# Two expert layers: the overflow branch ahead of the tiles, the last tile mixed in by a product with a matrix of weights, the first tile's rows of the first layer by one-hot products

## The chip, the cores and the metric

The kernel runs on one core of a Trainium2 chip. The metric is the device time of one execution in microseconds (us). The engines are PE (matrix products; PEld is its loading of the stationary operand), DVE (vector operations), ACT (activations and copies, and a queue for transfers), POOL (here mostly gathers of rows) and SP (issues loads of weights). Each runs its own instructions in order and waits on the others through semaphores. 16 DMA engines move the data.

## The reference

The program is a residual stack on x (256 tokens by 768): four pairs of a graph layer and a feed-forward layer, each as x = x + layer(layernorm(x)). Only two feed-forward layers are touched. Both are mixtures of eight experts of which each token uses two:

```python
# L1_ffn, "first expert layer"
topk_vals, topk_idx = jax.lax.top_k(xf @ Wr.T, 2)
routing_weights = jax.nn.softmax(topk_vals, axis=-1)
h = jnp.einsum('th,efh->etf', xf, Wi) + bi[:, None, :]        # 768 -> 384
expert_out = jnp.einsum('etf,ehf->eth', gelu(h), Wo) + bo[:, None, :]
out = sum of routing_weights * expert_out over the token's two experts

# L2_ffn, "second expert layer"
w, idx = gate(xt, gate_w, gate_b)                              # two of eight, in groups
g = swiglu((x @ W1 + B1) * (x @ W3 + B3))                      # 768 -> 768 -> 384
out = sum of w * (g @ W2 + B2) over the token's two experts + shared_ffn(xt)
```

`shared_ffn` has the form of one more expert that every token uses.

## The kernel before

256 tokens with two experts each are 512 rows. Each expert computes only its own rows. How many an expert gets is known only at run time, so the experts are ranked by load (`ranked`, line 992) and put into a fixed set of tiles of 128 rows: `TILES1` (line 1189) has seven, `TILES2` (line 1190) six. Each entry is (rank, first row, rows): the most loaded expert has 192 rows, some tiles are shared by two experts of 64 rows. `plan` (line 966) gives for each rank where its rows begin (base), how many fit (room) and where they go if they don't (jump). Rows that don't fit go to further tiles, "more", which are computed only when some expert has more rows than room: the overflow branch, a `tc.If` on a number read from memory. With the given inputs it isn't taken.

`dispatch` (line 1024) works out on DVE the row number of each of a token's two experts (`places`), the matrix `is_e` of which expert has which rank, and hands back a function `rest` (line 1052) for what can wait: row numbers as integers, the two weights, the overflow flag. `find` (line 1076) turns this round: a one-hot matrix `hot` compares the row numbers with a count (four DVE operations), and PE products with the tokens' numbers give for each row of a tile its token (`slots`). `take` gathers the rows of a tile from a copy of the normalized x in DRAM (indirect DMA on POOL, `take_rows`, line 1101), and `tile_t` (line 1104) transposes them on PE.

The tiles then run in a loop (lines 1397 to 1414 for the first layer, 1623 to 1640 for the second). In one turn: the up products of tile u, the transposes of the activations of tile u-1 (`turned`), the transposes of tile u+1's rows, the down products of tile u-1 (`finish`, line 1162), whose result y goes to DRAM (`ys`) by ACT's queue (line 1165). All expert products are recorded at line 1117, in `by_parts`. Weights come in pieces of 1152 KB into a ring of eight buffers: `stream` (line 1170) with `pump` and `done` issues on SP (line 87) as many loads as there are free buffers. The expert's number is read from memory by SP (`nth`, line 1167). The second layer's W2 has a ring of three buffers of its own ("down").

After the loop: the last tile's `finish`; the expert's bias products (line 1419 in the first layer, `down_t`, lines 1095 and 1097, for the shared expert and the biases in the second) with `add_acc` (line 1324) into x; the overflow branch (lines 1423 and 1650); and `add_rows` (line 1127): four gathers from `ys` (two experts, two halves of the tokens), each multiplied by its weight and added to x (line 1134), and the layer norm of the next layer (lines 150 to 160). Then the next graph layer starts with transposes (line 171). After the second expert layer this graph layer also loads a small matrix `bd` by ACT's queue (line 1673), multiplies it on DVE (lines 1682, 1684) and uses it in `ps_a` (line 1692).

In the second layer the shared expert's up products (`up_shared(0)`, `(1)`, `(2)`; lines 102 and 1504 to 1513) stand ahead of the loop, between the steps of routing.

The order on each engine follows from the program by a scheduler that goes by priorities and ready times; products marked by `pin` keep the program's order among themselves. Across a `tc.If` nothing is moved: all that stands before it in the program is issued before it, all that stands behind it after it.

## Time and profile before

| | us |
|---|---|
| median of 4 runs (lowest, highest) | 1452.5 (1447.61, 1455.6) |
| the profiled execution: time | 1452.53 |
| its span in the profile | 1450.7 |
| PE busy in the span | 1246.9 |
| DVE, ACT, POOL busy | 665.2, 474.3, 357.2 |
| first expert layer: from its first tile's products to the next layer's first transpose | 861.69 to 948.54 |
| second expert layer: the same | 1095.36 to 1258.63 |

A line of the timeline gives the start in the span and the duration of an instruction or of a run of like ones (x is their number), the engine, the line of the kernel, the operation, the tile written, the tiles read, and their shape; in brackets how long the engine was idle before it and what ended that. A q behind the engine's name is its sequencer, which issues transfers and branches. An f32 product is recorded as two instructions. The table by stretches gives the granted clock of PE as a share of full speed and the mean share of the 16 DMA engines that was busy.

### The profile page before, as it was taken

How to read it: one execution, taken by the hardware profiler on the slowest of the kernel's cores; microseconds unless marked ns; L12 is line 12 of the kernel's file. 1: busy time of each engine (PE TensorE's matmuls, PEld its weight loads, DVE VectorE, ACT ScalarE, POOL GpSimd, SP SyncE). 2: the span in 40 equal slices, each digit the busy share in tenths (PEclk: the TensorE clock that was granted, in tenths of full speed). 3: DMA queues.
4: the chain of work that ended last, by engine and by line, in shares of the span. 5: the costliest groups of instructions: out<-in, count | busy, mean ns of one | idle time of the engine just before them, and what ended most of it. 6: DMA issues, size and time to landing. Idle time of an engine off the chain costs nothing. (4 is left out here: it accounts for less than half of the span.)

```text
span 1450.7 us, 13873 instructions
## 1 busy us (share of the span) xinstructions
PE 1246.9 (86%) x5047; PEld 768.8 (53%) x5068; DVE 665.2 (46%) x1251; ACT 474.3 (33%) x822; POOL 357.2 (25%) x195
## 2 busy tenths in 40 slices
PE   7999999789997884998989859676899999377998
PEld 4576444347643432855555445345486554166964
DVE  4321999930099996164352530166341101346023
ACT  1013877611287662241231112124111111153113
POOL 1001999900099991000203010111001000100000
PEclk9999999989999995999999969887989999665899
DMA  9323250205230023233632169461039995700000
GB/s 333 131 94 102 61 159 6 98 33 196 98 99 0 1 98 116 85 115 138 247 113 76 66 231 391 185 242 33 23 130 354 380 403 213 290 7 34 33 0 22
DMA packets 77930, 197.15 MB, mean 136 GB/s; under 512 B 9084, under 2 KB 24000, under 8 KB 77728
## 3 DMA queue, kind: packets, MB, share of 16 engines
q1 hardware_dynamic: 69088, 162.28, 31.1%
q0 software_dynamic: 6304, 27.94, 5.5%
q10 hardware_dynamic: 2464, 5.96, 1.1%
q8 instruction: 44, 0.72, 0.2%
q14 instruction: 30, 0.25, 0.1%
HBM read 177.84 MB, written 14.87 MB: 133 GB/s over the span
## 5 line engine op out<-in xcount | busy, mean ns | idle before, releaser
L784 POOL TENSOR_TENSOR gate<-gate,qT 128x2048 f32<-128x2048 f32 x64 | 287.7, 4531 | 241.7 <-ACT gate L764 241.3
L769 DVE TENSOR_REDUCE qiT<-gate 128x32 f32<-128x2048 f32 x96 | 215.0, 2279 | 16.2 <-POOL gate L784 15.1
L764 ACT ACTIVATE gate<-gate_acc,bg 128x1024 f32<-128x1024 f32 x192 | 209.6, 1113 | 38.2 <-PE gate_acc L760 35.5
L759 PE MATMUL gate_acc<-sela,ga 128*128 128x512 bf16 x363 | 139.3, 384 | 25.2 <-ACT gate L764 24.5
L760 PE MATMUL gate_acc<-selb,gb 112*128 112x512 bf16 x384 | 147.8, 385 | 1.2
L1117 PE MATMUL up_acc<-w_e,xgT 128*64 128x384 f32 (+1 forms) x432 | 96.5, 489 | 0.0
L760 PEld LDWEIGHTS <-gb 112*128 112x128 bf16 x384 | 37.6, 98 | 96.2 <-issue 71.3
L791 DVE TENSOR_TENSOR gate<-gate,ps_qy 128x2048 f32<-128x2048 f32 x32 | 72.9, 2278 | 0.2 <-ACT gate L764 0.2
L1117 PEld LDWEIGHTS up_acc<-w_e,xgT 128*64 128x64 f32 (+1 forms) x432 | 46.8, 154 | 44.9 <-issue 27.3
L171 PE MATMUL ps_tr<-ident,xn 128*128 128x128 f32 x84 | 18.0, 381 | 53.6 <-DVE ln_rs L158 27.0
L759 PEld LDWEIGHTS <-ga 128*128 128x128 bf16 x384 | 37.8, 98 | 47.8 <-issue 2.2
L642 PE MATMUL ps_alpha<-w_qb,qiT 128*128 128x384 f32 x96 | 44.1, 553 | 19.8 <-DVE qiT L769 19.8
L1101 POOL DMA_INDIRECT yg<-ys,rows x8 | 7.6, 953 | 196.6 <-PEq L1650 137.2
L566 DVE TENSOR_TENSOR ps_hg<-ps_hg,hg 128x384 f32<-128x384 f32 x8 | 4.5, 562 | 107.9 <-ACT hg L565 107.9
L326 PE MATMUL ps_pt<-ident,gat_z 128*128 128x128 f32 x104 | 24.2, 370 | 30.4 <-DVE gat_s L318 30.4
L457 PE MATMUL ps_z<-w_rel,xT 128*128 128x384 f32 x144 | 47.9, 486 | 0.0
L457 PE MATMUL ps_z<-w_rel,nT 128*128 128x384 f32 x144 | 47.5, 489 | 0.0
L461 ACT COPY z<-ps_z 128x384 f32<-128x384 f32 x24 | 11.5, 478 | 104.4 <-PE ps_z L457 104.4
L171 PEld LDWEIGHTS ps_tr<-ident,xn 128*128 128x128 f32 x84 | 14.5, 198 | 58.4 <-issue 33.5
L267 DVE CUSTOM_DVE_ANT_0 gat_dot<-xl,row 128x128 f32<-128x128 f32 (+2 forms) x56 | 23.8, 424 | 46.6 <-ACT xl L1471 18.9
L152 ACT ACTIVATE ln_rs<-ln_mv,eps_t 128x1 f32<-128x1 f32 x24 | 7.1, 295 | 111.6 <-DVE ln_mv L151 107.9
L1602 DVE TENSOR_TENSOR h<-up_acc,h 128x768 f32<-128x768 f32 x6 | 5.7, 958 | 80.0 <-PE up_acc L1117 80.0
(425 smaller groups left out, 2220.1 us busy)
## 6 DMA issues: line engine op xcount, KB each, us to landing
w_e<-in_L_ffn_W SPq DMA_DIRECT2D x32, 1152.0 KB, 12.3
w_rel<-in_L_gnn_W_rel SPq DMA_DIRECT2D x12, 1152.0 KB, 11.3
wi<-in_L_ffn_WiT SPq DMA_DIRECT2D x8, 1152.0 KB, 16.0
wo<-in_L_ffn_WoT SPq DMA_DIRECT2D x8, 1152.0 KB, 13.7
w_down<-in_L_ffn_W SPq DMA_DIRECT2D x8, 1152.0 KB, 12.2
ys<-y ACTq DMA_DIRECT2D x13, 384.0 KB, 6.0
w_root<-in_L_gnn_W_root SPq DMA_DIRECT2D x4, 1152.0 KB, 12.6
w_ga<-in_L_gnn_WgAT SPq DMA_DIRECT2D x4, 1152.0 KB, 6.2
```

What stands on the lines that cost most here:

```text
L171: nc.tensor.transpose(ps[:, j, :], src[:, c, (k + j) * P:(k + j + 1) * P], ident)
L267: pin(nc.vector.tensor_tensor_reduce(t, xl[:, c, h * C:(h + 1) * C], r[:, h * C:(h + 1) * C], 1.0, 0.0, OP.mult, OP.add, accum_out=a2[:, w ...
L326: pin(nc.tensor.transpose(ps[:, j, s, :], zs[h, d][:, j, s * P:(s + 1) * P], ident))
L457: mm = nc.tensor.matmul(ps, hT[:, k, c * P:(c + 1) * P], w(k, i * 384, (i + 1) * 384), start=k == 0, stop=k == KD - 1)
L642: pin(nc.tensor.matmul(al_ps[c][i], qiT[:, f, c * P:(c + 1) * P], w(f, i * 384, (i + 1) * 384), start=False, stop=f == KD - 1))
L759: pin(nc.tensor.matmul(acc[:, i, :], ga[:, b, fs], sela, start=True, stop=False))
L760: pin(nc.tensor.matmul(acc[:, i, :], gb[0:112, u, b, fs], selb[0:112, i], start=False, stop=True))
L764: pin(nc.scalar.activation(g[:, u * 16:(u + 1) * 16, :].rearrange("p n l -> p (n l)"), acc.rearrange("p a n -> p (a n)"), AF.Sigmoid, bias ...
L769: pin(nc.vector.tensor_reduce(qiT[:, f, b * NPB:(b + 1) * NPB], g, AX.X, OP.add))
L784: pin(nc.gpsimd.tensor_tensor(g, g, q[:, None, :].to_broadcast([P, NPB, LQ]), OP.mult))
L791: pin(nc.vector.tensor_tensor(g, g, q_ps[:, None, :].to_broadcast([P, NPB, LQ]), OP.mult))
L1117: pin(nc.tensor.matmul(ps[at:at + n, :], xT[:, k, at:at + n], ws[r](k, lo, hi), start=start, stop=stop))
```

## The change

- The overflow branch of both layers moves from behind the tiles to ahead of them. In the first layer it stands behind the first tile's rows, ahead of the first weight loads (`pump`) and of `find`. In the second it stands behind `up_shared(1)`, ahead of `pump`, `find` and `up_shared(2)`; loads in its body use the ring of three. The overflow flag is worked out early in `dispatch`.
- The first tile of the first layer gets its rows, already transposed, by products of the normalized x with a one-hot matrix of 128 columns (`first_rows`): four DVE operations, twelve products of 128x128, two copies. `find` there covers the other six tiles only.
- The last tile's y is no longer written to DRAM. `rest` builds a matrix, 128 rows of the last tile by 256 tokens, with the weight of each row for each token (four DVE comparisons with a multiplication, an addition, two transposes, a copy). Four products of it with y (`end_tiles`) are added in PSUM onto the bias products, and one `add_acc` for each half of the tokens takes all of it into x.
- `add_rows` gathers the other tiles' rows as before, but stands ahead of the last tile's `turned` and `finish`; a token's row in the last tile is replaced by row 0 with weight 0. The norm moves into `end_tiles`.
- In the second layer the order behind the loop is now: gathers, shared expert's down products for the first half, `turned`, those of the second half, `finish`, mix. The array in DRAM is filled with zeros for one tile more.

```diff
         of = tmp([P, 3, 8], "of_expert")
         nc.vector.tensor_reduce(of, q, AX.X, OP.add)
+        full = tmp([P, 8], "over_e")
...
+        nc.vector.tensor_copy(over, any_f)
         base, room, jump = (of[:, i, None, :].to_broadcast([P, NC, 8]) for i in range(3))
...
-        def rest(cw):
-            rows = tmp([P, NC, 2], "rows", I32)
-            nc.vector.tensor_copy(rows, places)
+        def rest(cw, last):
...
+            rel = tmp([P, NC, 2], "row_rel")
+            nc.vector.tensor_scalar(rel, places, float(last * P), None, op0=OP.subtract)
+            mix = neg1.rearrange("p c (j n) -> p c j n", j=2)
+            for c in range(NC):
+                for j in range(2):
+                    nc.vector.tensor_scalar(mix[:, c, j, :], count_up[:, :P], rel[:, c, j:j + 1], weights[:, c, j:j + 1],
+                                            op0=OP.is_equal, op1=OP.mult)
+            nc.vector.tensor_tensor(mix[:, :, 0, :], mix[:, :, 0, :], mix[:, :, 1, :], OP.add)
+            ps = bank("ps_mix")[:, :N]
+            for c in range(NC):
+                nc.tensor.transpose(ps[:, c * P:(c + 1) * P], mix[:, c, 0, :], ident)
+            mixT = cnt1[:, 0, :]
+            nc.scalar.copy(mixT, ps)
+            kept = tmp([P, NC, 2], "row_kept")
...
+            nc.vector.tensor_tensor(rows, places, kept, OP.mult)
+            return rows, weights, mixT
...
+    def first_rows(pool, places, name):
+
+        at = pool.tile([P, NC, P], F32, name="first_at")
+        for c in range(NC):
+            nc.vector.tensor_scalar(at[:, c, :], count_up[:, :P], places[:, c, 0:1], None, op0=OP.is_equal)
+            nc.vector.scalar_tensor_tensor(at[:, c, :], count_up[:, :P], places[:, c, 1:2], at[:, c, :],
+                                           op0=OP.is_equal, op1=OP.add)
+        t = pool.tile([P, KD, P], F32, name=name)
+        for k in range(0, KD, 3):
+            ps = bank("ps_xg")[:, :384].rearrange("p (k n) -> p k n", k=3)
+            for j in range(3):
+                for c in range(NC):
+                    pin(nc.tensor.matmul(ps[:, j, :], xn[:, c, (k + j) * P:(k + j + 1) * P], at[:, c, :],
+                                         start=c == 0, stop=c == NC - 1))
+            nc.scalar.copy(t[:, k:k + 3, :], ps)
+        return t
...
+    def end_tiles(accs, y, mixT):
+
+        xn = normed()
+        for c in range(NC):
+            for i in range(2):
+                pin(nc.tensor.matmul(accs[c][:, i, :384], mixT[:, c * P:(c + 1) * P], y[:, i * 384:(i + 1) * 384],
+                                     start=False, stop=True))
+            add_acc(accs[c], c)
             norm(x, xn, D, c)
         return xn
...
-        pump()
-        places, is_e, rest = dispatch(f1, plans[0], mask, before, total, is_r)
-        slots = find(f1, places, 0, len(TILES1), "slots1")
...
+        places, is_e, over, rest = dispatch(f1, plans[0], mask, before, total, is_r)
...
+        xgT = first_rows(f1, places, "first_xgT")
         count = nc.values_load(over[0:1, 0:1], min_val=0, max_val=1, **UNCHECKED)
         with tc.If(count > 0, preferred_fallthrough_block=False):
...
+            index.clear()
+        pump()
+        slots = find(f1, places, P, len(TILES1) - 1, "slots1")
...
+        add_rows(gathered, ys, rows1, w1s)
+        gT = turned(f1a, last)
+        accs = []
+        for c in range(NC):
+            accs.append(acc2("moe_acc"))
+            for i in range(2):
+                pin(nc.tensor.matmul(accs[c][:, i, :384], cwT[:, c * P:(c + 1) * P], bo[:, i * 384:(i + 1) * 384],
+                                     start=True, stop=False))
+        xn = end_tiles(accs, finish(f1a, None, gT, views(parts, "wo"), parts), mixT)
...
-        pump()
-        up_shared(1)
-        places, is_e, rest = dispatch(f2, plans[1], mask, before, total, is_r)
-        slots = find(f2, places, 0, len(TILES2), "slots2")
-        nc.vector.tensor_tensor(cw, cw, mask, OP.mult)
...
+        up_shared(1)
+        count = nc.values_load(over[0:1, 0:1], min_val=0, max_val=1, **UNCHECKED)
+        with tc.If(count > 0, preferred_fallthrough_block=False):
...
+        pump()
+        slots = find(f2, places, 0, len(TILES2), "slots2")
         xg = take(slots[:, 0:1])
+        nc.vector.tensor_tensor(cw, cw, mask, OP.mult)
         up_shared(2)
...
+        add_rows(gathered, ys, rows2, w2s)
         ws2 = views([("s", 0, P)], "2")["s"]
...
-        xn = add_rows(gathered, ys, rows2, w2s)
+        accs = []
+        for c in range(NC):
+            accs.append(acc2("moe2_acc"))
+            down_t(accs[c], gs, ws2, c, cwT, b2)
+            if c == 0:
+                gT = turned(f2a, last)
+        xn = end_tiles(accs, finish(f2a, None, gT, views(parts, "2"), parts), mixT)
```

## The prediction

> **What bounds the kernel now.** I first read the busy table: PE is busy for 1246.9 us of 1450.7 (86%), every other engine for less than half. The chain that ended last is headed by PE too. So a change is worth what it adds to PE's work or takes from PE's gaps. Next I read the timeline (start, duration, engine, line, operation, tiles, and in brackets the idle time before and what ended it) at the four places where the diff touches PE: the front and the tail of each expert layer.
>
> The front of the first expert layer:
>
> ```profile
> 848.98 0.40 SPq L87 DMA_DIRECT2D wi<-in_L_ffn_WiT  x1
> 850.43 0.16 DVE L1050 TENSOR_SCALAR places<-row_ends 128x2 f32<-128x2 f32 x1
> 850.50 1.53 DVE L1080 TENSOR_SCALAR hot<-count_up,places 128x896 bf16<-128x896 f16 x4
> 853.41 1.03 POOL L1101 DMA_INDIRECT xg<-table,slots  x1 [15.32 <-DVE slots L1088]
> 860.07 1.52 PE L1109 MATMUL ps_xg<-ident,xg 128*128 128x128 f32 x6 [7.14 <-DMA xg<-table,slots]
> 861.69 4.48 PE L1117 MATMUL up_acc<-wi,xgT 128*128 128x384 f32 x9
> ```
>
> Once `places` is known, PE waits 7.14 us for the gathered rows. Its first expert product starts at 861.69; behind it the tiles follow without a gap. The weights were asked for at 848.98, before the branch existed on SP.
>
> Its tail:
>
> ```profile
> 928.27 2.84 PE L1419 MATMUL moe_acc<-bo,cwT 8*128 8x384 f32 x8
> 932.10 0.95 POOL L1101 DMA_INDIRECT yg<-ys,rows  x1 [57.55 <-SPq L1423]
> 939.74 1.02 DVE L1134 SCALAR_TENSOR_TENSOR x<-yg,row_w,x 128x768 f32<-128x768 f32 x1 [7.63 <-DMA yg<-ys,rows]
> 948.54 2.79 PE L171 MATMUL ps_tr<-ident,xn 128*128 128x128 f32 x12 [17.43 <-DVE ln_rs L158]
> ```
>
> PE is idle for 17.43 us: branch, gathers, adds, norm.
>
> The front of the second expert layer, where PE has no gap to fill:
>
> ```profile
> 1083.04 0.74 PE L1085 MATMUL ps_slot<-token,hot 128*128 128x1 bf16 x24
> 1083.64 10.61 PE L102 MATMUL ps_e<-xT,w_s 128*128 128x256 f32 x48
> 1085.17 0.42 DVE L1513 TENSOR_TENSOR gs<-gs,sgm 128x256 f32<-128x256 f32 x1
> ```
>
> Its tail:
>
> ```profile
> 1221.75 3.01 PE L1095 MATMUL moe_acc<-w_down,gs 128*128 128x384 f32 x6 [2.06 <-DMA w_down<-in_L_ffn_Ws]
> 1242.46 0.95 POOL L1101 DMA_INDIRECT yg<-ys,rows  x1 [137.21 <-PEq L1650]
> 1250.14 1.02 DVE L1134 SCALAR_TENSOR_TENSOR x<-yg,row_w,x 128x768 f32<-128x768 f32 x1 [7.04 <-DMA yg<-ys,rows]
> 1258.12 1.17 ACTq L1673 DMA_DIRECT2D bd<-in_L_gnn_WT  x2
> 1258.63 1.51 PE L171 MATMUL ps_tr<-ident,xn 128*128 128x128 f32 x6 [16.53 <-DVE own L1676]
> 1263.38 0.55 DVE L1682 TENSOR_TENSOR of_row<-row,bd 64x384 f32<-64x384 f32 x1 [2.83 <-DMA bd<-in_L_gnn_WT]
> 1268.27 2.05 PE L1692 MATMUL ps_a<-own,xT 128*128 128x4 f32 x9 [6.06 <-DVE own L1684]
> ```
>
> PE waits 16.53 us, then 6.06 more for `bd`. Last, the table by stretches (after each engine's busy time: granted clock, DMA share, GB/s):
>
> ```profile
> 850.00:862.00 12.00, 3.32 (x36) 2.83 (x37) 2.89 (x19) 0.86 (x2) 4.06 (x5) 0.50 1.02 358
> 1096.00:1220.00 124.00, 123.68 (x582) 63.06 (x580) 15.46 (x34) 17.93 (x37) 1.41 (x2) 1.00 0.95 363
> 1256.00:1262.00 6.00, 2.81 (x12) 2.28 (x12) 3.44 (x10) 1.61 (x5) 0.00 (x0) 0.50 1.03 400
> ```
>
> In the first and third, PE runs at half clock and the DMA engines are full; in the second both PE and the DMA are full.
>
> **Step 1, first layer, front.** Removed: PE's 7.14 us wait for xg. Added: four DVE operations of 128x128 (the shorter L1149 copies of 128 columns take 0.22, the L1080 ones of 896 columns 0.38; say 0.25 each, so from 850.4 to 851.4), then 12 f32 products of 128x128 and two copies to SBUF (0.48 each). At half clock a 128x128 f32 record takes 1.51/6 = 0.25 in the ps_tr row, but that is a transpose with one pass; the nearest real f32 product of that size is L1705's, 2.84 us for 24 records at full clock, 0.118 each, so 0.24 at half clock, and each product here is two records: 24 x 0.24 = 5.7. PE reaches the branch at 851.4 + 5.7 = 857.1. The branch is new at this point, and it is a join: in the tail SP did nothing between its load at 900.2 and 931.67, when PE had passed. So the first weight load, which now stands behind the branch, moves from 848.98 to about 857.4 (+8.4). On an empty DMA queue the earliest wi landed 5.7 us after issue: 863.1 instead of 861.69, +1.4. find, tile 1's gather and `rest` also stand behind the branch, but tile 1's rows are not needed before 868. The first products start after the clock has been idle again, so about 1 us more goes at half speed. Later weight pieces: at 3 us each (1152 KB at 390 GB/s) the fifth, which tile 2 needs, lands near 857.4 + 15 + 2.7 = 875, and tile 2 would start at 879: covered; without that cover each microsecond is one of PE's. **Taken: +2.5** (ends +0.5: the first load lands with no clock penalty and PE passes sooner; +6: the products take twice the row and push the branch by 3.5 more).
>
> **Step 2, first layer, tail.** Removed: the last tile's write and the branch ahead of the gathers. Added: eight mix records (2.84 by the 8-record row above), two add_acc of 0.96 behind the gathers instead of ahead of them. The gathers now wait for tile 5's write, issued at 923.84. SP, no longer held by the branch, issues the next layer's loads as buffers come free: three from tile 5's finish at 923.3, two from 928.3. So this write lands under full DMA, near the median of 6.0: first gather about 929.9 instead of 932.10, 2.2 earlier. Landing is still under load: 7.6 as before. DVE gains 2.2, then does two adds of 0.96 more at the end: ps_tr at about 948.0 for 948.54. **Taken: -0.5** (ends -8: write and gathers land unloaded, 2.3 the shortest write, and the mix sets the end: the same products end at 931.1, copy 0.5, first half of the mix 1.4, add and norm some 5.5, about 938.5, 10 earlier, less 2 for a gather still behind a load; +1: one load more lies ahead of a gather).
>
> **Step 3, second layer, front.** Before, find's DVE and PE work lay inside up_shared: PE went from one to the next in 0.6 us. After, up_shared(1) comes first, then the branch, then find, then up_shared(2). up_shared(1)'s products still end at 1083.1. DVE, in order, first does the layer's gating operations up to 1085.59; DVE, PE, SP and ACT meet at the branch (0.3 to 0.6 from load to next operation in the tail); hot at 1086.3 takes 1.5 (1.53 for 7 tiles), the last slot product ends at 1088.1. up_shared(2) starts there instead of at 1083.64: 4.5 later, all on PE's path, since nothing else is ready for PE. Then the clock: PE has been idle for some 3 us. At 1219.7 an idle time of 2.06 was followed by a clock of 0.50 until about 1229.7; at 860.03 full clock came 4.6 after the restart. Work of 4.6 us at half clock is 2.3 lost; up to 3.4 with the longer one. `rest` now adds two transposes on PE, 0.25. SP's first w_e, 1076.64 before, goes to about 1084; its landing near 1096 by the median 12.3 still precedes the first tile, now at 1102. **Taken: +7.5** (ends +4.5: clock kept; +9.5: full loss and a slower branch). [...]
>
> **Step 4, second layer, tail.** Removed from behind the last product: the last y write, the branch, the gathers' 7 to 8 us. The gathers go out during the last tile, once tile 4's write has landed (about 1223), and land by 1236.5: hidden under PE's work, which ends with the mix near 1244; that cover is 6 us. Order on PE now: down_t(0), turned, down_t(1), finish; it ends at 1241.5 as the same products do now, copy 0.48, first half of the mix to 1242.9, second to 1244.2; add_acc 0.96, statistics 1.0, 0.2, 0.3, 0.15, norm 0.52 and queueing: ps_tr at about 1248.6 instead of 1258.63, -10.0. Behind it stands `bd`: its load, 5.2 from issue to use under a DMA share of 1.03. SP's stream (11.8 MB from about 1217 at 390 GB/s) is over near 1246.5, so bd, issued near 1248.1, lands in about 2.3, as small loads elsewhere did in 1.8 to 2.6. ps_a at 1255.2 for 1268.27. **Taken: -13** (ends -10: bd keeps 5.2; -14: it lands in 1.8 and its DVE work packs).
>
> **A branch's own price.** ACT went on 0.39 to 0.6 after its load, SP 0.1 to 0.5 after PE. PE's own price is not shown: its compare-branch rows of 3.4 and 4.0 us are the draining of its products. I take 0.5, already inside steps 1 and 3; the far end is 4.0 each. [...]
>
> Zero-filling one more tile (384 KB each, at the program's start, line 1209) costs nothing: only the gathers, hundreds of microseconds later, wait for it.
>
> **Sum.** +2.5 - 0.5 + 7.5 - 13 = -3.5. The profiled execution is 1452.53 (span 1450.7 plus 1.8), and the median of the runs 1452.5, so the sum stands against either: 1449.0. The measurement can tell 0.5%, 7.3 us, from no change.
>
> **Rivals.** *The tail is freed of loads too* (faster): the first layer's last write and gathers land unloaded, -8 for step 2, total -11: 1441.5. For it: DMA share is only 0.12 to 0.16 from 910 to 924. Against: the loads the branch held are let go into just this stretch.
> *The first weights land late* (slower): the first wi takes the median 16.0 instead of the shortest 5.7, because all eight pieces are asked for within a few us of each other and share the 16 engines. It costs 10.3 more: +6.8, 1459.3. From a landing of 9.2 the whole change is a loss. For it: 16.0 is the median of eight; against: the first of the queue landed in 5.7 with the same company behind it.
> *The change does not shift the last wait*: PE's second tail still ends at bd under full DMA because SP's loads, no longer held by the branch, are there as well: -10, and with a slower branch at the front +9.5: sum +1.5, 1454.
>
> **How the numbers follow.** My forecast, within a few us of 1449, 0.50; the faster rival 0.24; the late weights 0.16; the unshifted wait 0.10. Range: 1439 to 1460, from the faster rival with 2.5 more to the slower one; the forecast's own is 1444 to 1455. Faster by over 0.5% (under 1445.2): the faster rival and a sixth of the forecast, 0.31. Slower (over 1459.8): half of the late weights, with a branch nearer 4.0 on PE, 0.16. Same: 0.53.
>
> **What would show it.** Step 1: first product at line 1117 about 2.5 later relative to the router; first wi issued 8 later. Step 2: the gap ahead of ps_tr still near 16. Step 3: PE's gap of about 5 between the two up_shared, half clock after it. Step 4: gathers ended before the last product, gap ahead of ps_tr about 4 instead of 16.5, bd landed in 2 to 3. It is wrong if PE waits at a branch for more than 1 us with all others there, or if a tile waits for weights.

## The result and the profile after

| | before | after |
|---|---|---|
| median (lowest to highest), us | 1452.26 (1444.13 to 1461.28, 78 runs) | 1454.91 (1446.07 to 1461.08, 52 runs) |
| profiled execution: time, span | 1452.53, 1450.7 | 1452.09, 1450.3 |
| PE busy | 1246.9 | 1260.8 |

The ratio of after to before is 1.0018, with a 95% interval from 1.0008 to 1.0027: some 2.6 us slower, where 3.5 us faster was forecast. Single runs of one kernel lie up to 17 us apart, so the profiled execution of after can be the shorter one by chance. So each kernel has a second profile (the experiments `before2` and `after2`), and the table below gives both, first and second. The stages follow each other without a gap, from the last step of routing in the first expert layer (the DVE operation that writes `known`, just ahead of `places`) to the end of PE's work.

| stage | before, us | after, us | difference of the means | forecast |
|---|---|---|---|---|
| first layer: `known` to first expert product | 16.06, 15.95 | 16.15, 17.46 | +0.8 | step 1: |
| first layer: its tiles, to the last up product | 56.42, 56.41 | 61.43, 62.49 | +5.5 | +2.5 for both |
| first layer: tail, to the next transposes | 30.43, 30.33 | 29.97, 29.95 | -0.4 | step 2: -0.5 |
| graph layer, to the first `up_shared` product | 111.23, 111.37 | 105.42, 105.78 | -5.7 | 0 |
| second layer: front, to the first expert product | 35.59, 37.26 | 45.15, 45.55 | +8.9 | step 3: +7.5 |
| second layer: its tiles, to the last up product | 124.32, 124.32 | 124.21, 124.21 | -0.1 | 0 |
| second layer: tail, to `ps_a` | 48.59, 45.70 | 33.88, 34.04 | -13.2 | step 4: -13 |
| from `ps_a` to the end | 177.78, 175.36 | 184.29, 184.02 | +7.6 | 0 |

The sum is +3.4; 0.6 less went by ahead of `known`, which leaves +2.8, close to the difference of the medians (2.65). Two of the eight places moved although the diff does not touch them, in opposite directions.

The timeline of after at the places that the prediction showed of before (start, duration, engine, line, operation, tiles; in brackets the idle time and what ended it):

```profile
855.54 0.41 SPq L87 DMA_DIRECT2D wi<-in_L_ffn_WiT  x1
859.15 0.59 PE L1378 MATMUL ps_cw<-ident,router_l 128*8 128x128 f32 x2 [3.73 <-issue]
861.26 1.02 POOL L1120 DMA_INDIRECT xg<-table,slots  x1 [23.30 <-DVE own L1193]
861.66 7.18 PE L1153 MATMUL up_acc<-wi,first_xgT 128*128 128x384 f32 x12 [0.55 <-DMA wi<-in_L_ffn_WiT]
871.13 0.86 PE L1153 MATMUL up_acc<-wi,xgT 128*64 128x384 f32 x2 [1.37 <-ACT xgT L1129]
873.09 4.08 PE L1153 MATMUL up_acc<-wi,xgT 128*64 128x384 f32 x22 [1.09 <-DMA wi<-in_L_ffn_WiT]
...
936.59 0.95 POOL L1120 DMA_INDIRECT yg<-ys,rows  x1 [57.06 <-PE moe_acc L1176]
953.06 2.18 PE L171 MATMUL ps_tr<-ident,xn 128*128 128x128 f32 x9 [14.86 <-DVE xn L160]
...
1051.80 2.44 PE L209 MATMUL ps_router<-router_w,xT 128*128 128x8 f32 x12 [0.38 <-ACT xT L172]
1054.42 1.54 PE L171 MATMUL ps_tr<-ident,xn 128*128 128x128 f32 x6 [0.18 <-DVE xn L160]
1055.90 2.73 PE L209 MATMUL ps_router<-router_w,xT 128*128 128x8 f32 x12
...
1086.19 1.41 DVE L1099 TENSOR_SCALAR hot<-count_up,places 128x768 bf16<-128x768 f16 x4 [1.32 <-DVEq L1667]
1088.85 0.78 PE L1104 MATMUL ps_slot<-token,hot 128*128 128x1 bf16 x24 [6.36 <-DVE own L1193]
1089.49 12.39 PE L102 MATMUL ps_e<-xT,w_s 128*128 128x256 f32 x48
...
1231.88 0.95 POOL L1120 DMA_INDIRECT yg<-ys,rows  x1 [118.46 <-DMA w_a<-in_L_ffn_AT]
1253.00 2.40 PE L171 MATMUL ps_tr<-ident,xn 128*128 128x128 f32 x12 [3.92 <-DVE xn L160]
1257.00 1.14 DVE L1738 TENSOR_TENSOR of_row<-row,bd 64x384 f32<-64x384 f32 x2 [3.27 <-DMA bd<-in_L_gnn_WT]
1261.72 5.25 PE L1748 MATMUL ps_a<-own,xT 128*128 128x4 f32 x24 [6.33 <-issue]
...
1402.44 0.70 PE L225 MATMUL lg_acc<-kT,aT 64*128 64x256 f32 x4 [2.17 <-ACT at_p L232]
```

What to see in it. In the first layer, PE stands still for 3.73 us behind the branch, with "issue" as the reason: it waits for nothing that another engine does. The weights are asked for at 855.54; the first product starts at 861.66, where before it was 861.69, but it takes 7.18 us for 5.45, and the second tile then waits 1.37 for its rows and 1.09 for weights. The gap ahead of the next layer is 14.86. In the second layer, PE is idle for 6.36 us between the two `up_shared`, and `hot` was done at 1087.6, before PE came back at 1088.85. In its tail the gathers are out at 1231.88, long before the last product, and the gap ahead of `ps_tr` is 3.92 in place of 16.53.

The branch's own rows (for each line: shortest/mean/longest of its two records in ns, and their first and last start) explain the two idle times. They are on PE's sequencer; first of before, then of after:

```profile
L1423 PEldq COMPARE_BRANCH  x2: 98/1749/3400, 927.3 to 931.3; - x2
L1650 PEldq COMPARE_BRANCH  x2: 81/2034/3987, 1237.1 to 1242.3; - x2
```

```profile
L1439 PEldq COMPARE_BRANCH  x2: 98/1736/3375, 853.4 to 855.6; - x2
L1667 PEldq COMPARE_BRANCH  x2: 81/3042/6002, 1079.4 to 1082.7; - x2
```

The second record of after begins at 855.6 and lasts 3.38 us, to 859.0, and PE's next product starts at 859.15. In the second layer it begins at 1082.7 and lasts 6.00, and PE's next product starts at 1088.85. PE has nothing to drain at these places: its last products ahead of them ended at 855.41 and 1082.49. In before the same record was as long, and its last product in the first tail had ended too, at 931.11 (the row at 928.27 of 2.84); but there PE had to wait for the gathers and the norm anyway.

### The profile page after: what moved, and what is told of

The parts are those of the page before. It is cut to its first block, busy times and chain, and to the rows that moved or that the text cites. A ratio compares the mean times of both kernels' runs of the same rounds, so it can differ in the third digit from the quotient of the medians.

```text
span 1450.3 us, 13968 instructions
## 1 busy us (share of the span) xinstructions
PE 1260.8 (87%) x5081; PEld 777.7 (54%) x5102; DVE 670.2 (46%) x1273; ACT 477.0 (33%) x825; POOL 356.4 (25%) x194
## 5 line engine op out<-in xcount | busy, mean ns | idle before, releaser
L627 PE MATMUL ps_alpha<-w_qa,gT 128*128 128x384 f32 x96 | 39.9, 498 | 0.0
L338 PE MATMUL gat_acc<-xl,gat_pt 128*128 128x128 f32 (+2 forms) x128 | 35.1, 432 | 5.3 <-DVE gat_s L347 5.3
## 6 DMA issues: line engine op xcount, KB each, us to landing
wi<-in_L_ffn_WiT SPq DMA_DIRECT2D x8, 1152.0 KB, 15.7
wo<-in_L_ffn_WoT SPq DMA_DIRECT2D x8, 1152.0 KB, 15.2
```

Of the source, the lines that this page charges most:

```text
L338: pin(nc.tensor.matmul(accs[d][:, i, at:at + wide], pts[h, d][:, j, s, :], xl[:, s, lo:lo + wide], start=s == 0, stop=s == NC - 1))
L627: pin(nc.tensor.matmul(al_ps[c][i], hT[:, k, c * P:(c + 1) * P], w(k, i * 384, (i + 1) * 384), start=k == 0, stop=False))
```

## Experiments

Two theories of PE's late start behind the branch stood against each other. One is the join (A, where a quoted text uses letters): the engines meet at the branch, and PE goes on when the last has come. The other is the fetch of code (D): the branch jumps over the long body, and PE's instructions behind it must be brought in first.

### Which layer, and what the branch is worth

**First layer alone.** The second layer is as before (its branch and `add_rows` behind the last tile again), the first as changed.

```diff
+        pump()
+        up_shared(1)
+        places, is_e, over, rest = dispatch(f2, plans[1], mask, before, total, is_r)
+        slots = find(f2, places, 0, len(TILES2), "slots2")
+        nc.vector.tensor_tensor(cw, cw, mask, OP.mult)
...
-        up_shared(1)
-        count = nc.values_load(over[0:1, 0:1], min_val=0, max_val=1, **UNCHECKED)
-        with tc.If(count > 0, preferred_fallthrough_block=False):
...
```

> Only the first expert layer is changed; the second is as before. Theory A (each branch ahead of the tiles is a join that holds work, the tails gain): the first layer alone costs what the two traces show up to the next layer's first transpose, +5.0 in the tiles and -0.5 in the tail, so 4.5 us slower than before, a ratio of 1.003. Theory B (the fronts matter little; what the tail of the second layer gains is given back later by PE's clock in the last layers): within 1.5 us of before. Theory C (the difference of the medians is made by the graph layers in between, whose length differs by 5.8 us in the two traces): faster by 1 or more.

Measured: 1455.64, ratio 1.0021 [0.9996, 1.0045]. Its first layer's front, in the timeline:

```profile
862.53 6.71 PE L1164 MATMUL up_acc<-wi,first_xgT 128*128 128x384 f32 x12 [4.77 <-DMA wi<-in_L_ffn_WiT]
...
871.52 0.86 PE L1164 MATMUL up_acc<-wi,xgT 128*64 128x384 f32 x2 [1.47 <-ACT xgT L1140]
874.44 5.78 PE L1164 MATMUL up_acc<-wi,xgT 128*64 128x384 f32 x22 [2.06 <-DMA wi<-in_L_ffn_WiT]
```

Here PE passed the branch in 0.58 us (a record of the instruction queue, the profile's q8, begins at 853.54 already, 2.0 us ahead of the branch; what was in it isn't recorded), and still nothing was gained: the first product waited 4.77 for its weights, which were asked for at 855.43, and the second tile waited 2.06 for its own. So in the first layer two things stand behind the branch at once, the code and the weights; taking away one leaves the other. From `known` to the last up product it took 17.14 + 63.61 = 80.8, against 72.4 before.

**Second layer alone.** The mirror image: the first layer as before (branch and `add_rows` behind the last tile again), the second as changed.

```diff
-        xgT = first_rows(f1, places, "first_xgT")
-        count = nc.values_load(over[0:1, 0:1], min_val=0, max_val=1, **UNCHECKED)
-        with tc.If(count > 0, preferred_fallthrough_block=False):
...
+        xg = take(slots[:, 0:1])
+        rows1, w1s = rest.old(cw)
+        xgT = tile_t(f1a, xg, "xgT")
...
```

> Only the second expert layer is changed; the first is as before. Theory A: +8.7 in front of the tiles, -14.7 from the last product of the tiles to ps_a, so 6 us faster than before (0.996). Theory B: the tail's gain is given back behind it, so 0 to 3 us slower. Theory C: 0 to 6 us faster, but with a graph layer between the two expert layers that is as long as before's 111 us.

Measured: 1455.4, ratio 1.0019 [0.9996, 1.0041]. The front of the second layer took 53.4, more than in after, because a second stop follows the first:

```profile
1093.38 0.66 PE L1076 MATMUL ps_mix<-ident,neg 128*128 128x128 f32 x2 [7.24 <-issue]
...
1099.08 0.62 PE L1115 MATMUL ps_slot<-token,hot 128*128 128x1 bf16 x18 [4.91 <-issue]
```

The records of the instruction queue (16,384 bytes each) begin at 1090.75 and at 1096.60, each about 2.5 us before PE goes on: two fetches, one after the other. The graph layer between the two expert layers took 110.98 here and 105.68 in `first_only`: its -5.7 goes with the first layer's change.

**No branch.** Both branches are taken out of after, and with them the computing of rows beyond the tiles (of the diff, the first layer's part).

```diff
-        count = nc.values_load(over[0:1, 0:1], min_val=0, max_val=1, **UNCHECKED)
-        with tc.If(count > 0, preferred_fallthrough_block=False):
-            slots = find(f1, places, len(TILES1) * P, len(more), "slots1_more")
...
```

> The changed kernel without both overflow branches (that part is left out; the given inputs never take it). Theory A: the first layer's weights are asked for at once and PE's gap in the second layer's front goes, so 4 to 5 us of the first front and 6 to 7 of the second come off the changed kernel: 8 to 10 us faster than before (0.994). If the branches cost only their own instructions (0.5 us each): 1 us off the changed kernel, so 1 to 2 us slower than before. Theory B: at most 2 us faster than before.

Measured: 1442.67, ratio 0.9922 [0.9892, 0.9951]. From `known` to the last up product of the first layer 73.4 for 78.8 in after (mean of two), and the front of the second layer 36.8 for 45.4 (the profile is of the slowest of six runs, 1449.67). By these stages the branch ahead of the tiles, with all that had to stand behind it, is worth 5.4 and 8.5 us. The 73.4 is still above the 72.4 of before, so making the first tile's rows by products gained nothing even without a branch.

**Work moved ahead of the branch.** The first layer's `pump` and the second layer's `find` come before the branch; the first body gets a buffer of its own, so that it doesn't use the ring.

```diff
+        pump()
         places, is_e, over, rest = dispatch(f1, plans[0], mask, before, total, is_r)
...
-                    loaded[r, kind] = load(r, kind)
+                    loaded[r, kind, "m"] = load_piece(f1a, a["L1_ffn_WiT" if kind == "wi" else "L1_ffn_WoT"][e], "w_more", "more", 1)
...
-        pump()
         slots = find(f1, places, P, len(TILES1) - 1, "slots1")
...
         up_shared(1)
+        slots = find(f2, places, 0, len(TILES2), "slots2")
         count = nc.values_load(over[0:1, 0:1], min_val=0, max_val=1, **UNCHECKED)
...
-        slots = find(f2, places, 0, len(TILES2), "slots2")
```

> The changed kernel with the same branches, but the first layer's weight loads ahead of the branch (its body has a buffer of its own), and the second layer's find ahead of the branch, so that up_shared(2) can follow it at once. Theory A: nearly the gain of leaving out the branches: first wi asked for near 849 instead of 855.5, PE's gap between the two up_shared about 1 us instead of 6; 7 to 10 us faster than before (0.994). If the loss lies in the branch itself (code to be fetched, engines meeting) and not in what is queued behind it: as the changed kernel, 2 to 3 us slower than before.

Measured: 1451.62, ratio 0.9995 [0.997, 1.0021]. The weights were asked for at 849.53, and the first layer's two stages fell to 15.10 + 58.80 = 73.9, 4.9 less than after. In the second layer nothing was gained (45.5), although PE had only `up_shared(2)` to start behind the branch and nothing to wait for. The branch's rows, then PE's first work behind the second branch:

```profile
L1462 PEldq COMPARE_BRANCH  x2: 98/1518/2937, 854.3 to 856.3; - x2
L1691 PEldq COMPARE_BRANCH  x2: 73/3162/6252, 1080.7 to 1081.0; - x2
```

```profile
1087.41 12.05 PE L102 MATMUL ps_e<-xT,w_s 128*128 128x256 f32 x48 [7.11 <-issue]
```

### Join or fetch

**A short body.** As `early`, but both bodies hold only their `find`; the rest of the overflow's computing is left out. The branch, the reading of the flag and all meetings of engines at it stay (of the diff against `early`, the second layer's part).

```diff
         with tc.If(count > 0, preferred_fallthrough_block=False):
             slots_m = find(f2, places, len(TILES2) * P, len(more), "slots2_more")
-            for j, r in enumerate(more):
...
```

> As the run early, with the branches where they are, but their bodies hold only find: what computes the overflow rows is left out (the given inputs never take it), so that PE jumps over some 50 instructions instead of hundreds. Theory D (PE waits after the branch for the code behind it, under the weight loads): its idle times put down to issue right behind the branches, 3.3 us in the first and 7.1 us in the second layer of the run early, fall below 1.5 us; PE's clock is kept in the second layer, and the way from the first up_shared product to the first expert product there falls from 45.5 to about 37 us; 8 to 11 us faster than before. Theory A (engines meet at the branch): both idle times stay, and so does the time of the run early, 1 us faster than before.

Measured: 1444.97, ratio 0.9939 [0.9915, 0.9963].

```profile
L1462 PEldq COMPARE_BRANCH  x2: 93/202/310, 856.9 to 858.4; - x2
L1683 PEldq COMPARE_BRANCH  x2: 69/124/179, 1083.0 to 1083.3; - x2
```

```profile
1083.56 10.63 PE L102 MATMUL ps_e<-xT,w_s 128*128 128x256 f32 x48 [0.93 <-PEq L1683]
```

With the same branch at the same place and under the same loads, PE's record is 0.18 instead of 6.25, its idle time 0.93 instead of 7.11, and the clock stays up (10.63 for 12.05). No record of the instruction queue begins around this branch (none between 1068.66 and 1087.55). The front of the second layer is 38.65 instead of 45.5. That is the theory of the join refuted and that of the fetch shown for the second layer. In the first layer the two stages took 73.48 for 73.9, only 0.4 less; but `early`'s fetch there was a short one (2.94), and with a long one the same code takes 77.3 (see `late_w`).

**A version meant to be better.** As `early` in the first layer, but with the first two tiles' rows gathered into tiles of their own ahead of the branch, instead of `first_rows`; the second layer as changed.

```diff
-        xgT = first_rows(f1, places, "first_xgT")
+        slots = find(f1, places, 0, len(TILES1), "slots1")
+        xgs = [f1.tile([P, D], F32, name=f"xg{i}") for i in range(2)]
+        for i in range(2):
+            take_rows(xgs[i], table, slots[:, i:i + 1])
...
         with tc.If(count > 0, preferred_fallthrough_block=False):
...
+        xgT = tile_t(f1a, xgs[0], "xgT")
```

> The changed kernel, but in the first layer the weights are asked for ahead of the branch, and the first two tiles' rows are gathered as before instead of being made by products; the branch stands behind these gathers, in the 7 us in which PE waits for them anyway. Theory D: the code is fetched inside that wait, the first expert product stands where it stood before (16 us after known), the tiles take 56 us as before; the shorter graph layer behind (105.5 instead of 111) and the second layer stay as in the changed kernel: 5 us faster than the changed kernel, 2 to 5 faster than before. Theory A: the meeting holds the next gathers and the first product, and the gain is under 2 us.

Measured: 1452.7, ratio 1.0005 [0.9985, 1.0025]: a miss, no gain.

```profile
L1469 PEldq COMPARE_BRANCH  x2: 98/3004/5910, 853.8 to 854.1; - x2
```

```profile
861.25 1.51 PE L1139 MATMUL ps_xg<-ident,xg 128*128 128x128 f32 x6 [7.83 <-DMA xg<-table,slots]
...
872.63 4.09 PE L1164 MATMUL up_acc<-wi,xgT 128*64 128x384 f32 x24 [1.47 <-ACT xgT L1140]
```

The fetch of 5.91 does lie inside the wait of 7.83 for rows, as meant. But the first product then comes at 864.03, the first tile runs mostly at half clock (6.31 us for 5.45), and the second tile waits 1.47 for its rows: 17.88 + 58.61 = 76.5 against 72.4 before. The second layer's price (45.3) stays.

**The second profiles.** Both kernels once more, unchanged, to see which differences repeat.

> The kernel before once more, for a second profile. If the last stage's 42.9 us (from the first lg_acc to the last product; 48 in the five others) and the graph layer's 111 us between the expert layers belong to the kernel, both come again; where one doesn't, it was chance of that execution and no part of the difference.

> The changed kernel once more, for a second profile: how far its stages repeat. Theory A and D: first expert layer's tiles near 61 us, the graph layer behind near 105.5, the way from up_shared to the first expert product near 45, from the last product of the tiles to ps_a near 34; what differs by more than 2 us is chance.

Measured: 1449.87 and 1455.35; the stages are in the table of the result. They repeat within 1.7 us but for two: `ps_a` to the end of before (177.78, 175.36) and its last tail (48.59, 45.70). The fetch in the second layer's front was 6.66 in after2.

### What sets the fetch, and where it costs nothing

**Weights asked for later.** As `early`, but the second layer's first weight loads wait for an operation of DVE that stands behind the branch.

```diff
             index.clear()
+        held_who = f2.tile([P, 8], I32, name="held_who")
+        nc.vector.scalar_tensor_tensor(held_who, gs[:, 1, :8], 0.0, who, op0=OP.mult, op1=OP.add)
+        who = held_who
         pump()
```

> As the run early, but in the second layer SP's first weight loads wait for a number that DVE makes behind the branch, so that the DMA engines are idle while PE passes the branch. Theory D2 (the code comes by DMA and queues behind the weights): PE's idle time behind the branch falls from 7.1 to about 3.5 us, as in the first layer, and the 16 KB record of the instruction queue starts about 1 us after the branch instead of 3.8. If the load of the DMA engines doesn't matter: 6 to 7 us again. The time of the whole is not the point, since the first tile may now wait for its weights.

Measured: one run of 1442.8.

```profile
L1691 PEldq COMPARE_BRANCH  x2: 81/1672/3262, 1084.4 to 1084.7; - x2
```

```profile
1088.15 13.54 PE L102 MATMUL ps_e<-xT,w_s 128*128 128x256 f32 x48 [4.13 <-DVE own L1215]
```

The DMA share in the 3 us behind the branch fell from 1.03 to 0.10, and PE's record from 6.25 to 3.26. The front was 44.06 for 45.5: half of the 3 us went into a longer time at half clock (13.54 for 12.05). So in the second layer the weights' stream accounts for the difference between the short and the long fetch. The low total comes from elsewhere: from `ps_a` to the end it took 175.1, where after took 184, a difference that is taken up below.

The first layer of `late_w` is the same code as that of `early`, with the same load on the DMA engines (shares of 1.05 and 1.04), and still its fetch took 6.24 us instead of 2.94:

```profile
L1462 PEldq COMPARE_BRANCH  x2: 98/3166/6235, 854.4 to 856.6; - x2
```

The record of the instruction queue begins 3.7 us behind the branch (860.30) where in `early` it began 0.5 behind it (856.75), PE goes on 6.4 us behind the branch instead of 3.1, and the two stages take 18.41 + 58.89 = 77.3 us for 73.9. Asking for the weights ahead of the branch thus brings 4.9 us or 1.5, by which fetch comes. What decides between the two isn't recorded.

**The branch where PE waits anyway.** The first layer's front is again as before, the gathers and the mix stay as changed, and both branches stand behind the mix, ahead of the norm. If taken, the body adds its rows by gathers of its own, so the overflow is still handled. The diff shows the first layer's part; the second layer's is alike.

```diff
-        xgT = first_rows(f1, places, "first_xgT")
-        count = nc.values_load(over[0:1, 0:1], min_val=0, max_val=1, **UNCHECKED)
...
+        end_tiles(accs, finish(f1a, None, gT, views(parts, "wo"), parts), mixT)
+        count = nc.values_load(over[0:1, 0:1], min_val=0, max_val=1, **UNCHECKED)
+        with tc.If(count > 0, preferred_fallthrough_block=False):
...
+            add_rows(gathered, ys, *beyond())
+        xn = norm_both()
...
```

> The changed kernel's mix and early gathers, but the overflow branch of both layers stands behind the mix, ahead of the norm, and its body adds the overflow rows to x by gathers of its own; the first layer's front is the one of before, with the weights ahead. Theory D: the code is fetched in the tails, where PE waits for the norm anyway: first layer's front and tiles as before (16 and 56 us), graph layer 105.5, second front 36, from the last product of the tiles to ps_a some 34 to 38 (fetch of 6 us in a wait of 4), the last stage 48: sum of the stages 8 us under before, 1444. If instead the meeting of the engines in the tail costs what it did in before: 2 us faster than before at most.

Measured: 1445.64, ratio 0.997 [0.9958, 0.9982]: 0.3% faster than before. The median of after was 1454.91.

```profile
L1506 PEldq COMPARE_BRANCH  x2: 98/2669/5240, 928.3 to 929.7; - x2
L1742 PEldq COMPARE_BRANCH  x2: 81/1684/3287, 1235.4 to 1236.8; - x2
```

```profile
944.67 2.79 PE L171 MATMUL ps_tr<-ident,xn 128*128 128x128 f32 x12 [15.21 <-DVE ln_rs L158]
1241.48 2.79 PE L171 MATMUL ps_tr<-ident,xn 128*128 128x128 f32 x12 [4.84 <-DVE ln_rs L158]
```

The fetches of 5.24 and 3.29 are still there, inside waits that end with the norm. Both fronts are those of before (16.06 + 55.91 and 36.8), and the last tail is 39.2, against 47.1 before and 34.0 in after: of the 13.2 that step 4 brought, 5 are given back, and the fronts are 6.8 and 8.5 shorter than those of after. Most of the 5 isn't the branch: behind a wait of 2.39 us PE runs at half clock from 1215.2 to 1222.1, which loses 3.4, where both profiles of after keep the clock at that place. The scheduler put some work that follows a branch in the program ahead of it: here SP loads the next layer's weights from 901.07 on, and its branch comes at 927.4; in after an operation of DVE of line 1451 runs at 846.27, ahead of its branch at 853.8. So the sentence in the description of the kernel that nothing is moved across a `tc.If` is too strong.

### The fetch in all profiles

The longer record of each branch on PE, in us, and the DMA share in the 3 us behind its start:

```
record  share   kernel and place
0.18    1.03    short, second layer (body short)
0.31    1.08    short, first layer (body short)
0.58    0.60    first_only, first layer (a queue record begins 2.0 ahead of it)
2.94    1.04    early, first layer
3.26    0.10    late_w, second layer
3.28    0.55    before2, first tail
3.29    0.12    tail_if, second tail
3.38    0.66    after, first layer
3.38    0.53    second_only, first tail
3.40    0.51    before, first tail
3.69    0.56    after2, first layer
3.99    0.63    before, second tail
4.10    0.64    first_only, second tail
4.21    0.64    before2, second tail
5.24    1.06    tail_if, first tail
5.91    1.04    best, first layer
6.00    0.97    after, second layer
6.22    1.02    best, second layer
6.24    1.05    late_w, first layer
6.25    1.03    early, second layer
6.66    0.98    after2, second layer
6.88    1.01    second_only, second layer
```

With a DMA share of 0.66 or less the fetch takes 3.3 to 4.2 us, with all engines busy 5.2 to 6.9 in eight of nine rows, and next to nothing where the body is short. (The row of 0.58 is `first_only`'s, with its early record in the instruction queue.) That queue's record tells which part grows: in after's first layer it begins 1.0 us after the branch (855.6 to 856.56), in its second 3.6 (1082.7 to 1086.32); from there PE takes 2.5 in both. So the fetch seems to wait in line behind the weights, and `late_w` and `early` differ by just that in the second layer. It doesn't always: in the nine rows under a full stream the queue's record begins between 0.5 us (`early`, first layer) and 4.4 us (`second_only`) behind the branch.

## Why the prediction was wrong, point by point

**A branch's own price: the step that failed.** The prediction read before's compare-branch rows of 3.4 and 4.0 us as "the draining of its products" and took 0.5, with 4.0 as the far end. They were the price itself, hidden in before by the gathers' 7 us; the prediction's own row at 928.27 has no product left to drain at 931.3. Its sign of being wrong, a wait of PE at a branch of more than 1 us, came in both layers, and a tile waited for weights as well. Moved ahead of the tiles, it is 3.38 and 3.69 in the first layer and, under the weights' stream, above the far end in the second: 6.00 and 6.66. `short` shows what it hangs on: 0.18 for 6.25 when the body that PE jumps over is short.

**Step 1, +2.5 forecast, +6.3 measured.** The weights were asked for at 855.54, sooner than the 857.4 of the working, and the first product came in time. SP had passed the branch itself at 850.6; its first load waited for PE to pass, by the table of waits (who waited for whom: us in total, times, longest):

```profile
SPq L87 <- PEq L1439: 3.9, 1, 3.9
```

The failed part is "tile 1's rows are not needed before 868: covered", and with it the look at the fifth weight piece alone. The rows were asked for at 861.26, since the slots wait for PE behind the fetch, and PE waited 1.37 for them. And the second tile is shared by two experts (ranks 0 and 7): the weights of rank 7 are the third piece, asked for at 857.14 and used at 873.09, 15.9 later, where the profile's table of transfers has a median of 15.7 for `wi`; PE waited 1.09. Tile 0 at half clock added 1.7. How much of the 6.3 is the weights and how much the fetch can't be split, since they hide each other: late weights with hardly a fetch (0.58) make 80.8 us (`first_only`), early weights with a fetch of 6.24 make 77.3 (`late_w`), with one of 2.94 or none 73.9 and 73.5, and after has 78.8. The rival of late weights had the right cause at the wrong piece: it priced the first, which was on time. The twelve products themselves were taken too long, 5.7 us for a measured 4.44.

**Step 2, -0.5 forecast, -0.4 measured.** Right in the sum, not in its two terms: the first gather went out 13.5 us behind the last up product (923.09 to 936.59), where 11.8 was forecast and 14.0 was before, and the rest of the way to `ps_tr` took 16.5 as before (16.4), where 1.7 more was forecast. The rival of an unloaded tail (-8) fell: the write that the gathers wait for was issued at 928.82, and the first gather's rows were taken up at 943.60, 7.0 after it.

**Step 3, +7.5 forecast, +8.9 measured.** The size was near, the mechanism wrong. The forecast had DVE's `hot` set PE's restart; DVE was done at 1087.6, and in `early` nothing was left to wait for, at the same 45.5. The fetch holds PE, and the idle time then costs clock: `up_shared(2)` takes 12.39 instead of 10.6, with half clock from 1086.28 to 1093.11. `second_only` shows that it can be dearer (53.4): a second fetch, with a stop of 4.91.

**Step 4, -13 forecast, -13.2 measured.** The mechanism was right, with the gathers hidden and a gap of 3.92 ahead of `ps_tr` (about 4 forecast). That the size fits so well is luck, since two errors cancel. `ps_tr` comes 25.1 us behind the last up product, where 28.9 was forecast: the forecast carried over the half clock that before's first profile has there, behind a wait of 2.06. Before's second profile keeps the clock behind a longer wait, and its tail is 45.70 for 48.59:

```profile
1224.61 2.17 PE L1095 MATMUL moe_acc<-w_down,gs 128*128 128x384 f32 x6 [2.25 <-DMA w_down<-in_L_ffn_Ws]
```

And `bd` was not free of the loads: the DMA share is 1.03 from 1245 to 1253, `bd` takes 3.9 us from issue to use (2.3 forecast, 5.3 before), and DVE waits 3.27 for it. PE waits 6.33 for `ps_a`, because that product's operand ends at 1261.63; what the row calls "issue" is this wait. So the gain is 14.6 against before's first profile and 11.7 against its second.

**What was taken as nothing, 1: the graph layer, -5.7.** The prediction's sum has no term for a place that the diff doesn't touch. The scheduler's order of work behind the first layer is another one. In before, the router's 24 products stand behind all twelve transposes of the normalized x; in after, the first half's products lie between the two halves of the transposes, and fill the wait for the second half's norm (3.05 before; the lines of after are at 1051.80 to 1055.90 above). Of before:

```profile
1053.45 1.54 PE L171 MATMUL ps_tr<-ident,xn 128*128 128x128 f32 x6 [3.05 <-DVE xn L160]
1054.79 5.13 PE L209 MATMUL ps_router<-router_w,xT 128*128 128x8 f32 x24
```

From those transposes to `up_shared` it takes 10.24 to 10.25 in before, before2, second_only and short, 7.89 to 7.91 in the eight others: 2.35 us. Of the rest, 1.6 lie in the attention part, where eight transposes moved to its end, 1.2 behind it and 0.6 ahead of it. `short` has the old order there and the attention part is shortest of all (58.5 for 61.2 and 59.6), so those transposes are not the reason. The order goes with the change in the first layer (only `short` has that change and the old order); why these 3.4 us went stays open.

**What was taken as nothing, 2: the last stage, +7.6.** Its work is the same in both kernels, but PE's clock is not. Both have an idle time of 2.17 us in front of the same product (of before it ends at 1407.60; of after, at 1402.44, the last line of the timeline above). What follows, by stretches (busy time of the engines, clock, DMA share, GB/s), first before, then after:

```profile
1408.00:1414.00 6.00, 6.00 (x32) 3.87 (x30) 3.71 (x11) 2.33 (x9) 0.00 (x0) 0.78 0.00 0
1414.00:1420.00 6.00, 6.00 (x36) 3.47 (x36) 4.17 (x10) 3.42 (x12) 0.00 (x0) 1.00 0.00 0
```

```profile
1408.00:1414.00 6.00, 6.00 (x22) 3.71 (x23) 2.47 (x5) 2.62 (x10) 0.00 (x0) 0.50 0.00 0
1414.00:1420.00 6.00, 6.00 (x22) 3.04 (x18) 2.59 (x5) 1.16 (x3) 0.00 (x0) 0.50 0.00 0
```

In before the half clock lasts 3.4 us, in after 17.1, which makes 42.9 and 48.0 us of the part from the first `lg_acc` to the end. In the traces of before and after, all changes of the clock lie on a grid of 3.413 us (the 42 and 44 stretches of one clock begin whole multiples of it apart, to 0.003 us); where the half clock is short, the idle time ends 0.2 to 0.3 us into a step of the grid (0.33 in before), where it is long, 2.1 to 2.3 (2.13 in after). Nine profiles have the long one, three the short: before, before2 and `late_w`, which has after's tail. So it is no property of the old tail, but of when the idle time falls. The wait ahead of the shared expert's down products in the second tail (2.06 to 2.51 us) fits the same grid: in before 2.06 us of it lie in one step, and half clock from 1222.94 to 1229.77 follows; in after 1.80, and the clock stays full. In the last stage the largest parts in one step are 1.83 in before and 2.13 in after, and half clock follows both. Over both places of all twelve profiles, a step with 1.83 us or more of the idle time in it is followed by half clock in the next step (18 of 18), and where no step has more than 1.80, the clock stays full (6 of 6). Why the half clock then lasts one step of the grid or several, up to five, was not found. How often it falls which way in runs without a profile was not measured, and so how much of the medians' difference it makes stays open. Of the 7.6, 5.2 are this; the other 2.4 lie ahead of it, where before's own two profiles differ by 2.4.

**The balance.** Step 1 and step 3 together cost 15.2 for a forecast 10.0, steps 2 and 4 brought 13.6 for 13.5. By the four places alone the change would be 1.6 slower: the branch's price, 5.4 and 8.5 by `noif`, is all of step 4's gain. Of the 6.3 us between the forecast sum (-3.5) and that of the stages (+2.8), 3.8 lie in step 1, 1.4 in step 3 and 1.9 in the two places taken as nothing (-5.7 and +7.6); the rest is -0.8. The rival of the unshifted wait named 1454, near the measured 1454.91, with a dear branch in the front, which came, and a second tail of only -10. It left out the two untouched places as well, so its number is luck. In the chances, the terms given for "faster by over 0.5%" add up to 0.32, not 0.31.

## What to carry to other kernels

Before a branch is moved, read its own long compare-branch record on PE: where PE's idle time right behind it was put down to "issue" (3.73 us in after, 7.11 in `early`), it was the fetch of code here, and it was free only as long as a wait for data lay over it. Put a conditional with a long body where the engines wait anyway (`tail_if`, whose fetches of 5.24 and 3.29 lie inside such waits) and, given the choice, away from a weight stream (`late_w`: 3.26 for 6.25). What a short jump is worth is shown by `short`, which leaves the body out; a version that keeps the body elsewhere was not run. When loads are delayed, check every piece's own first use, not only the first and the last one; compare a kernel's untouched stages too, since they moved by -5.7 and +7.6 here; and take two profiles before a wait of some 2 us is priced, since the clock behind it can fall either way (2.06 in before was followed by 6.8 us at half clock, 2.25 in `before2` by none).

## What the runs showed of the hardware that was not expected

- PE's record of a branch over a long body lasts 3.3 to 4.2 us with a DMA share of 0.66 or less (0.58 in `first_only`'s first layer) and 5.2 to 6.9 under a full weight stream (2.94 in one row of nine, `early`'s first layer); over a short body 0.18 and 0.31 (`short`). The fetch has 16,384 bytes, and the branch's record on PE ends 2.3 to 3.1 us after that of the instruction queue begins (2.4 at both places of after). A second fetch can follow with a stop of its own (4.91 in `second_only`).
- Idle times of 2.06 us (before, second tail) and 2.17 us (last stage of before and of after) were enough for the clock to fall. It changes on a grid of 3.413 us in before and after, and what an idle time cost depended on where in the grid it fell: 3.4 us at half clock in before or 17.1 in after for the same 2.17, and none for 2.25 (`before2`) or 6.8 for 2.06 (before) in the second tail. At the two places that were compared in all twelve profiles, 1.83 us within one step was enough (before, last stage) and 1.80 was not (after, second tail).
- The record of the instruction queue can start ahead of the branch (`first_only`, 2.0 us) or well behind it: 0.9 to 1.7 us with a DMA share of 0.66 or less (0.9 in before's first tail, 1.0 in after's first layer), 0.5 (`early`, first layer) to 4.4 (`second_only`) under the weights.
